# The first stage of a four-layer graph network in written order: gathers in slots, 32-pair one-hots, convolution with count blocks as weights

## The chip, the cores and the metric

One core of a Trainium2 chip runs the whole program in one launch. The metric is the device time in microseconds; three runs of the kernel before gave 3601.79, 3602.45 and 3603.7, median 3602.45.

## The reference

The graph has 6250 nodes with 64 features and 206250 edges (100000 random ones in both directions and a loop at each node), sorted by destination. Four layers follow each other, each as `x = x + layer(relu(layernorm(x)), edges)`:

```python
h = jnp.maximum(_layernorm(x, axis=-1), 0.0)
x = x + _L0_gnn_ref(h, edge_index, W3, b3, W4, b4)   # two normalised convolutions, ReLU between
h = jnp.maximum(_layernorm(x, axis=-1), 0.0)
x = x + _L1_gnn_ref(h, edge_index)                   # one convolution
h = jnp.maximum(_layernorm(x, axis=-1), 0.0)
x = x + _L2_gnn_ref(h, edge_attr_64, src, dst, ...)  # gated messages over the edges
h = jnp.maximum(_layernorm(x, axis=-1), 0.0)
x = x + _L3_gnn_ref(edge_index, h)                   # three propagations, averaged

def _sgconv(x, W, b, src, dst, n):                   # the convolution of layer 0, loops added
    norm = dinv[s] * dinv[d]                         # dinv = 1/sqrt(degree)
    agg = jax.ops.segment_sum(norm[:, None] * x[s], d, num_segments=n)
    return agg @ W.T + b
```

The last line of each layer 0 convolution shows what the stage at issue has to do: multiply features by a matrix that counts edges, scale, and apply a weight matrix.

## The kernel before

**The matrix of counts.** Nodes are padded to 6272, in 49 blocks of 128 (`NB`), seven blocks to a chunk (`CB`, `W` = 896 nodes, `NC` = 7 chunks). The first stage turns the edge list into a dense matrix of how many edges go from each source to each destination, one byte (fp8) a count, and writes it to DRAM as `A[0]` to `A[6]`. All later convolutions multiply by `A`. The features are held as three bf16 parts whose sum is the fp32 value (`split`, `U3`, `V3`), so that a matmul with counts loses nothing.

**Its steps.** `fast` computes a key for every edge, `pair` (destination times 49 plus source block; source within its block), and stores it in DRAM as `pairs`. The destinations are taken two at a time: 3136 pairs of nodes in 25 groups (`GC`) of 128. For each group, a scan over a coarse list (`near`, L804) finds roughly where each pair's edges begin (`begin`); an indirect gather on POOL brings 101 edges from there (`near2`, L872); a second scan (L876, L878) gives the exact place (`exact_i`); a second gather brings the next 128 edges (`run`, L881); they become small bf16 `digits` (L885 on DVE, L887 on ACT), which TensorE transposes (`p_dig`, L890) and DVE copies to `key` (L891). Every nine groups, comparisons (`less`, L900) and matmuls give the degrees; these make a round trip through DRAM (`degs`, `by_block`) to become `deg_dst` and `norm0`.

**Builds and strips.** `build` takes 16 pairs (`GB`): DVE writes two one-hot tiles, `hd` (block of the source, 1568 elements) and `lo` (source in its block, 2048 elements), both at L852; 16 matmuls of `lo` as weights with `hd` moving (98 columns, L861) give counts in `p_a`, two groups of eight (`SG`); ACT writes each group to a strip as fp8 (L865). A strip is 448 destinations wide (`CW`) for all 49 source blocks, 14 builds (`NQ`) fill it, and there are 14 strips (`CS`). A full strip goes to `A`.

**The first convolution.** While strip s+1 is built, `convolve(s)` multiplies strip s: the weights are the feature parts (128 sources by 64 features), the strip is the moving operand of 448 columns, and the three parts go alternately to the two halves of the result's partitions (`spread`, L748), so that the array is used as two tiles of 128*64. A matmul with the identity adds the loop edges (L949). ACT takes the result out as `y` (L957). `hidden`, in steps spread between builds, turns a finished chunk back to nodes (`twice`, L964), scales it, applies W3, ReLU and W4, and writes `V3`, the input of the second convolution.

**What sets the order.** In this stage a scheduler places the instructions of every engine by its own estimates; the text of the program is only a starting point. The second and third convolutions (`gather`, L1042) and the edge stage run with a written order on some engines (`tc.manual_schedule`). `gather` loads `piece`s of `A` (seven blocks by 896) and uses its 128x128 blocks as weights, with the 192 feature columns of a block moving. Pools of tiles have a fixed number of buffers: `rpool` 3, `opool` (one-hots) 2, `spool` (strips) 3, `p_a` 2.

Of the kernel before, what the change touches and what calls it, by code (L numbers as in the profile page):

```python
# [8 lines left out]
F32 = mybir.dt.float32  # L9
# [7 lines left out]
P = 128  # L17
N = 6250
# [572 lines left out]
GB = 16  # L591
GQ = 2
CW = 448
CS = NP // CW
SG = 8
# [21 lines left out]
def fast(ctx, tc, bad, x, src, dst, edge_attr, W3, b3, W4, b4, w1, b1, w2, b2, Bw, Bb, Cw, Cb,  # L617
# [10 lines left out]
    def strip_of(s, bs):  # L628

        return A[s // 2][:, bs, s % 2 * CW:(s % 2 + 1) * CW]  # L630
# [121 lines left out]
    nc.scalar.dma_start(X, x.rearrange("(b p) f -> p b f", p=P))  # L752
# [3 lines left out]
    with ExitStack() as ph:  # L756

        ipool = ph.enter_context(tc.tile_pool(name="ipool", bufs=1, reuse_waits="tile"))
        with ExitStack() as first:
            dpool = first.enter_context(tc.tile_pool(name="dpool", bufs=1, reuse_waits="tile"))  # L760
# [3 lines left out]
            nc.scalar.dma_start(src_i, src.rearrange("(p k) -> p k", p=P))  # L764
# [5 lines left out]
            nc.sync.dma_start(looks.rearrange("(p i) -> p i", p=P), look)  # L770
            hi = dpool.tile([P, K1], I32, name="hi")
# [7 lines left out]
            none = dpool.tile([1, 2 * (EP + 512 - E)], F32, name="none")  # L779
            nc.vector.memset(none, float(2 ** 22))  # L780
            nc.sync.dma_start(pairs[E:, :].rearrange("(o e) t -> o (e t)", o=1), none)
# [15 lines left out]
        looked = ExitStack()  # L797
        npool = looked.enter_context(tc.tile_pool(name="npool", bufs=1, reuse_waits="tile"))
        near = npool.tile([P, NS], F32, name="near")
        nc.sync.dma_start(near, looks.partition_broadcast(P))  # L800
        for c0, c1 in ((0, 3), (3, 10), (10, GC)):
            for c in range(c0, c1):
                w = min(max(int(c * 2 * P * E / N / LOOK) - 22, 0), NS - SW)
                nc.vector.tensor_scalar(junk, near[:, w:w + SW], start_of[:, c:c + 1],  # L804
                                        float(w - 1), op0=OP.is_lt, op1=OP.add,
                                        accum_out=begin[:, c:c + 1])
            nc.vector.tensor_scalar(begin[:, c0:c1], begin[:, c0:c1], float(LOOK), 0.0,
                                    op0=OP.mult, op1=OP.max)
            nc.vector.tensor_copy(begin_i[:, c0:c1], begin[:, c0:c1])
        looked.close()  # L810


        rpool = ph.enter_context(tc.tile_pool(name="rpool", bufs=3, reuse_waits="tile"))
        opool = ph.enter_context(tc.tile_pool(name="opool", bufs=2, reuse_waits="tile"))
        spool = ph.enter_context(tc.tile_pool(name="spool", bufs=3, side="right", reuse_waits="tile"))
        wpool = ph.enter_context(tc.tile_pool(name="wpool", bufs=1, reuse_waits="tile"))

        key = ipool.tile([P, 2, GC * P], BF16, name="key")
        below = ipool.tile([P, 3, GC], F32, name="below")

        W3_sb = wpool.tile([P, D], F32, name="W3_sb")
        nc.scalar.dma_start(W3_sb, W3)
        W4_sb = wpool.tile([D, P], F32, name="W4_sb")
        nc.scalar.dma_start(W4_sb, W4)
        b3_c = column(b3, 1, "b3_c")
        b4_r = rows(b4, "b4_r")
        W3T = const.tile([D, P], F32, name="W3T")
        W4T = const.tile([P, D], F32, name="W4T")

        with ExitStack() as ps:  # L830
            psum = ps.enter_context(tc.tile_pool(name="ps0", bufs=1, space=PSUM, reuse_waits="tile"))
            p = psum.tile([P, SG, P], F32, name="p_a", bufs=2)
            nc.tensor.transpose(p[:D, 0, :], W3_sb, ident)
            nc.vector.tensor_copy(W3T, p[:D, 0, :])
            p = psum.tile([P, SG, P], F32, name="p_a", bufs=2)
            nc.tensor.transpose(p[:, 0, :D], W4_sb, ident[:D, :D])
            nc.vector.tensor_copy(W4T, p[:, 0, :D])

            H0 = ipool.tile([P, NB, D], F32, name="H0")
            for c in range(NC):  # L840
                normed(H0[:, blocks(c), :], X[:, blocks(c), :])

            NQ = CW // 2 // GB
            strips = {0: spool.tile([P, NB, CW], COUNT, name="strip")}

            def build(s, q):

                at = (s * CW // 2) + q * GB
                lo = opool.tile([P, GB // GQ, 128, GQ], BF16, name="lo")
                hd = opool.tile([P, GB // GQ, 2 * NB, GQ], BF16, name="hd")  # L850
                for t, of, k in ((hd, turns, 0), (lo, count, 1)):
                    nc.vector.tensor_tensor(  # L852
                        t, of.unsqueeze(1).to_broadcast(t.shape),
                        key[:, k, at:at + GB].rearrange("p (h j) -> p h j", j=GQ)
                        .unsqueeze(2).to_broadcast(t.shape),
                        op=OP.is_equal)
                for r in range(GB // SG):
                    p = psum.tile([P, SG, P], F32, name="p_a", bufs=2)
                    for j in range(SG):
                        g = r * SG + j  # L860
                        nc.tensor.matmul(p[:, j, :2 * NB], lo[:, g // GQ, :, g % GQ],  # L861
                                         hd[:, g // GQ, :, g % GQ], start=True, stop=True)
                    col = 2 * (q * GB + r * SG)

                    nc.scalar.activation(  # L865
                        strips[s][:, :, col:col + 2 * SG].rearrange("p b (j l) -> p b j l", l=2),
                        p[:, :, :2 * NB].rearrange("p j (b l) -> p b j l", l=2), AF.Copy,
                        saturate=False)

            for c in range(GC):  # L870
                near2 = rpool.tile([P, LOOK, 2], F32, name="near2")
                nc.gpsimd.indirect_dma_start(  # L872
                    out=near2.rearrange("p e t -> p (e t)"), out_offset=None, in_=pairs[:, :],
                    in_offset=bass.IndirectOffsetOnAxis(ap=begin_i[:, c:c + 1], axis=0))
                n = rpool.tile([P, 1], F32, name="n")
                nc.vector.tensor_scalar(junk[:, :LOOK], near2[:, :, 0], start_of[:, c:c + 1], 0.0,  # L876
                                        op0=OP.is_lt, op1=OP.add, accum_out=n)
                nc.vector.tensor_add(exact_i[:, c:c + 1], begin[:, c:c + 1], n)  # L878
            for c in range(GC):
                run = rpool.tile([P, P, 2], F32, name="run")  # L880
                nc.gpsimd.indirect_dma_start(  # L881
                    out=run.rearrange("p e t -> p (e t)"), out_offset=None, in_=pairs[:, :],
                    in_offset=bass.IndirectOffsetOnAxis(ap=exact_i[:, c:c + 1], axis=0))
                digits = rpool.tile([P, 2, P], BF16, name="digits")
# [8 lines left out]
                if 0 <= c - 3 < NQ:  # L893
                    build(0, c - 3)
# [705 lines left out]
```

## Time and profile before

| | |
|---|---|
| median of the runs | 3602.45 us |
| profiled execution | 4099.17 us, its span 4097.5 us |
| granted TensorE clock, mean | 0.849 |
| busy over the span | PE 77%, PEld 53%, DVE 48%, ACT 31%, POOL 41% |
| first stage (until the first matmul of the first `gather`) | 0 to 578.4 us |
| two gathers (layer 0's second half, layer 1) | 578.4 to 1020.7 us |
| edge stage with layer 3's first sums | from about 1044 us to about 3615 us |

The profiled execution is 14% longer than the runs without a profile, so lengths of stretches are compared with its own span. PE is TensorE's matmuls and PEld its weight loads; SPq and ACTq in the timeline are DMA issues on those engines. In the timeline each row has its start, its duration, the engine and line, the operation with output and inputs, and in brackets how long the engine had been idle and what ended that. A row with a count (x12) merges consecutive instructions.

### The profile page before, as it was taken

The page shows a single profiled execution, that of the slowest core. Times are in us where ns is not written, and L with a number is a line of the kernel's source. Part 1 is how long each engine was busy: PE and PEld are TensorE (multiplying, and loading weights), DVE is VectorE, ACT ScalarE, POOL GpSimd, SP SyncE. Part 2 cuts the span into 40 slices and gives each one's busy share as a digit, 9 for nine tenths or more (in the row PEclk, how much of TensorE's full clock was granted, in tenths as well). Part 3 has the DMA queues.
Part 4 walks back from the last instruction along what each step waited for, and adds up shares of the span by engine and source line. Part 5 has one row for each costly group of instructions (what it writes and reads, how often), then busy time and mean ns, then how long its engine had stood idle before and what let it go on. Part 6 is the DMA issues. An engine that isn't in the chain of part 4 may idle for free.

```text
span 4097.5 us, 59586 instructions
## 1 busy us (share of the span) xinstructions
PE 3166.7 (77%) x24393; PEld 2174.5 (53%) x24393; DVE 1979.9 (48%) x3899; ACT 1255.6 (31%) x2024; POOL 1667.0 (41%) x1889
## 2 busy tenths in 40 slices
PE   1799999999566657776767677766767776699999
PEld 1566679998233324433434333433334443459999
DVE  6899946322244445544445444554444454561111
ACT  1577740000233333333333333333333333320000
POOL 4100010000566656656665656666566566600000
PEclk9799999999677767788777877878777787799999
DMA  3233355653322222222222222222222222136664
GB/s 101 73 84 101 94 169 190 205 181 118 95 75 61 46 53 74 61 80 57 58 63 74 64 64 67 72 59 58 75 56 61 73 65 66 45 113 194 194 203 152
DMA packets 229312, 388.76 MB, mean 95 GB/s; under 512 B 137573, under 2 KB 139743, under 8 KB 228771
## 3 DMA queue, kind: packets, MB, share of 16 engines
q1 hardware_dynamic: 170420, 321.51, 25.1%
q0 software_dynamic: 55104, 60.65, 7.9%
q8 instruction: 193, 3.16, 0.3%
q10 hardware_dynamic: 3504, 2.70, 0.3%
q14 instruction: 91, 0.75, 0.1%
HBM read 340.47 MB, written 44.24 MB: 94 GB/s over the span
## 4 chain that ended last, share of the span: by engine, by line
PE 55%; DVE 15%; another core or an unknown queue 12%; issue 9%; ACT 7%; DMA 1%; POOL 1%; DVEq 0%; ACTq 0%; SPq 0%; POOLq 0%
PE p_acc L1042 18%; PE p_sum L748 11%; PE p_bc L1396 7%; PE p L1382 6%; PE p_a L861 4%; ACT h L1386 2%; PE p_s L1424 2%; DVE m L1405 2%; DVE m L1406 2%; DVE junk L1282 2%; PE p_bc L1392 2%; PE p_e L1378 2%; PE p_sum L1276 1%; DVE m L1407 1%
## 5 line engine op out<-in xcount | busy, mean ns | idle before, releaser
L1370 POOL DMA_INDIRECT v<-Vp_dram,src_g x1616 | 1592.5, 985 | 1307.2 <-issue 786.4
L1042 PE MATMUL p_acc<-U,piece 128*128 128x192 bf16 x9604 | 814.8, 246 | 0.0
L1042 PEld LDWEIGHTS <-piece 128*128 128x128 fp8e4 x9604 | 796.4, 98 | 11.5 <-issue 4.2
L1396 PE MATMUL p_bc<-BC,h 128*128 128x256 f32 x1616 | 575.3, 485 | 22.7 <-issue 21.3
L1282 DVE SCALAR_TENSOR_TENSOR junk<-p_sum,there 128x512 bf16<-128x512 f32 (+1 forms) x392 | 241.8, 617 | 412.4 <-remote 288.6
L1405 DVE TENSOR_TENSOR m<-gate,v 128x512 f32<-128x512 f32 x202 | 140.2, 694 | 617.8 <-ACT gate L1401 426.8
L1396 PEld LDWEIGHTS p_bc<-BC,h 128*128 128x128 f32 x1616 | 335.2, 230 | 177.7 <-issue 142.0
L1276 PE MATMUL p_sum<-ident_b,piece 128*128 128x128 bf16 x1372 | 161.1, 240 | 335.8 <-DVE junk L1282 268.6
L748 PEld LDWEIGHTS <-U 128*64 128x64 bf16 x4116 | 236.9, 113 | 320.6 <-issue 179.6
L1276 PEld LDWEIGHTS <-piece 128*128 128x128 fp8e4 x1372 | 120.3, 108 | 491.4 <-issue 475.3
L748 PE MATMUL p_sum<-piece,U 128*64 128x448 fp8e4 x2058 | 273.9, 385 | 95.0 <-issue 65.5
L865 ACT ACTIVATE strip<-p_a 128x784 fp8e4<-128x784 f32 x392 | 302.0, 820 | 126.2 <-PE p_a L861 110.0
L1382 PE MATMUL p<-h,w_d 128*128 128x512 f32 x404 | 269.1, 749 | 65.9 <-ACT h L1386 56.2
L1386 ACT ACTIVATE h<-p,b_c 128x512 f32<-128x512 f32 x404 | 262.1, 684 | 186.7 <-remote 75.5
L1052 DVE TENSOR_REDUCE zg<-p_acc 128x128 f32<-128x384 f32 x112 | 56.3, 507 | 523.4 <-PE p_acc L1042 522.9
L1469 ACT ACTIVATE m<-m 128x512 bf16<-128x512 f32 x202 | 127.3, 630 | 542.6 <-DVE m L1468 368.9
L1424 PE MATMUL p_s<-m,to 128*128 128x192 bf16 x1616 | 207.4, 279 | 99.6 <-DVE r_s L1432 56.2
L1392 PE MATMUL p_bc<-BC_b,ones 3*128 3x512 bf16 x404 | 182.2, 451 | 114.7 <-DVE m L1406 97.0
L1412 ACT ACTIVATE m<-m 128x512 bf16<-128x512 f32 x202 | 127.2, 630 | 433.9 <-DVE m L1407 319.3
L1382 PE MATMUL p<-eT,w_d 128*128 128x512 f32 x404 | 246.3, 694 | 13.0 <-ACT h L1386 8.0
L1392 PEld LDWEIGHTS <-ones 3*128 3x128 bf16 x404 | 37.5, 93 | 398.7 <-issue 223.3
L748 PE MATMUL p_sum<-strip,U 128*64 128x448 fp8e4 x2058 | 244.6, 360 | 2.5 <-ACT U L711 1.4
(198 smaller groups left out, 3441.3 us busy)
## 6 DMA issues: line engine op xcount, KB each, us to landing
piece<-A SPq DMA_DIRECT2D x249, 784.0 KB
e<-in_edge_attr SPq DMA_DIRECT2D x202, 256.0 KB
A<-strip SPq DMA_DIRECT2D x14, 2744.0 KB
v<-Vp_dram,src_g POOLq DMA_INDIRECT x1616
there<-A SPq DMA_DIRECT2D x28, 784.0 KB
pairs<-pair SPq DMA_DIRECT2D x1, 1616.0 KB
Vp_dram<-v SPq DMA_DIRECT2D x7, 224.0 KB
out<-X SPq DMA_DIRECT2D x6, 224.0 KB
```

Of the source, the lines that this page charges most:

```text
L748: nc.tensor.matmul(p[half * D:(half + 1) * D, :w], U3[:, b, k, :], at_block, start=(i < 2), stop=(i >= 3 * n - 2))
L865: nc.scalar.activation(strips[s][:, :, col:col + 2 * SG].rearrange("p b (j l) -> p b j l", l=2), p[:, :, :2 * NB].rearrange("p j (b l) -> ...
L1042: nc.tensor.matmul(p[d // 2][:, d % 2 * 3 * D:(d % 2 + 1) * 3 * D], t[:, b, d * P:(d + 1) * P], U3[:, k * CB + b, :, :].rearrange("p t f - ...
L1276: nc.tensor.matmul(p[:, a - a0, :], held["here", i, k][:, a, b * P:(b + 1) * P], ident_b, start=True, stop=True)
L1282: nc.vector.scalar_tensor_tensor(junk[:, :(a1 - a0) * P], p[:, :a1 - a0, :].rearrange("p a q -> p (a q)"), 15.5, of_there, op0=OP.min, op1 ...
L1370: nc.gpsimd.indirect_dma_start(out=v[:, j, :], out_offset=None, in_=Vp_dram[:, :], in_offset=bass.IndirectOffsetOnAxis(ap=src_g[:, g, j:j ...
L1382: nc.tensor.matmul(of[g][p], w, of[g].pop(x), start=True, stop=True)
L1386: nc.scalar.activation(of[g][t], of[g].pop(p), **how)
L1392: nc.tensor.matmul(p_bc[:, 4 * b:4 * b + 4].rearrange("p j o f -> p (j o f)"), ones, BC_b, start=True, stop=False)
L1396: nc.tensor.matmul(p_bc[:, 2 * q:2 * q + 2].rearrange("p j o f -> p (j o f)"), h2[:, q * P:(q + 1) * P], BC, start=False, stop=(k == 1))
L1405: nc.vector.tensor_mul(m, of[g].pop("gate"), of[g].pop("v"))
L1424: nc.tensor.matmul(p, to[:, :, j], m3[:, j].rearrange("p t f -> p (t f)"), start=(j == 0), stop=(j == J - 1))
```

## The change

The whole first stage becomes a function, `first_stage`, run with a written order on PE, DVE, ACT and POOL (SP stays with the scheduler).

- **Loads and start.** `src` is loaded on SP's queue, behind `dst`; X alone stays on ACT's. `near` is put into the buffer of a strip and is loaded right after `looks`. Edges beyond the end get a key out of range by arithmetic (`beyond`, `pads`), so that the store of `none` no longer overlaps `pairs`.
- **Slots.** One loop of 32 slots interleaves both gathers: slot i issues the first gather of group i, scans group i-2, issues the second gather of group i-3, makes the digits of i-5 and the key of i-6. Each slot then takes 1.4 units of `fill`: the remaining scans, the layer norms in three steps (the square on ACT), then single builds (`whole`).
- **One-hots for 32 pairs.** `one_hots(s, q, 2)` writes 3136 and 4096 elements in one instruction each (`GB` = 32); `placed` does its matmuls and evictions, in two portions of 16 pairs. The one-hots of the next job are written ahead of the placing of this one.
- **Strips.** A strip is now four or three blocks of a chunk (`OF_CHUNK`), 16 or 12 portions.
- **Convolution.** `convolve` works in units of two destination blocks (or one): the strip's 128x128 block is the weight, 192 feature columns move, as in `gather`; the identity adds the loops; DVE sums the three parts out of PSUM (`tensor_reduce`). `sums(n, built)` issues n such matmuls when the strip has been built that far. `hidden` takes nodes directly: four transposes of two blocks each, and W3T in both halves of the partitions.
- `H0` lies in the buffer that `V3` takes later; `norm3` is computed after the split of U3.

```diff
-GB = 16
+GB = 32
+OF_CHUNK = ((0, 4), (4, CB))
...
+        near = new_strip().rearrange("p b w -> p (b w)")[:, :4 * NS].bitcast(F32)
...
-            nc.scalar.dma_start(src_i, src.rearrange("(p k) -> p k", p=P))
+            nc.sync.dma_start(src_i, src.rearrange("(p k) -> p k", p=P))
+            nc.scalar.dma_start(X, x.rearrange("(b p) f -> p b f", p=P))
...
+            nc.sync.dma_start(near, looks.partition_broadcast(P))
...
+        def centred(c):
...
+            nc.scalar.activation(parts["q", c], h, AF.Square)
...
+        fill = [(0.4, scanned, c) for c in range(3, 10)] + [(0.3, begun_at, 3, 10)]
+        fill += [(0.4, scanned, c) for c in range(10, GC)] + [(0.3, begun_at, 10, GC)]
+        norms = []
+        for c in range(NC + 2):
+            norms += [(1.4, centred, c)] * (c < NC)
+            norms += [(0.6, deviation, c - 1)] * (0 <= c - 1 < NC)
+            norms += [(0.8, scaled, c - 2)] * (c >= 2)
+        for _, f, *args in norms[:3]:
+            f(*args)
+        fill += norms[3:]
+        for c in range(3):
+            scanned(c)
+        begun_at(0, 3)
+
+        near_of, run_of, digits_of, credit, singles = {}, {}, {}, 0.0, 0
+        for i in range(GC + 7):
+            if i < GC:
+                near_of[i] = rpool.tile([P, LOOK, 2], F32, name="near2")
                 nc.gpsimd.indirect_dma_start(
...
+            credit += 1.4
+            while credit > 0:
+                cost, f, *args = fill.pop(0) if fill else (2.0, whole, 0, singles)
+                singles += f is whole
+                f(*args)
+                credit -= cost
...
+                p = psum.tile([P, 512], F32, name="p_sum", bufs=2)
+                nc.tensor.matmul(p[:, :m * 3 * D], ident_b,
+                                 U3[:, at:at + m, :, :].rearrange("p b t f -> p (b t f)"),
+                                 start=True, stop=False)
+                for b in range(NB):
+                    for d in range(m):
+                        nc.tensor.matmul(
+                            p[:, d * 3 * D:(d + 1) * 3 * D],
+                            strips[s][:, b, (d0 - lo + d) * P:(d0 - lo + d + 1) * P],
+                            U3[:, b, :, :].rearrange("p t f -> p (t f)"),
+                            start=False, stop=(b == NB - 1 and d == m - 1))
...
+                nc.vector.tensor_reduce(
+                    zs[c][:, d0:d0 + m, :],
+                    p[:, :m * 3 * D].rearrange("p (d t f) -> p d f t", t=3, f=D),
+                    axis=AX.X, op=OP.add)
...
+        ready = one_hots(*jobs[0], 2)
+        for c in range(NC):
+            u = wpool.tile([P, CB, D], F32, name="z", bufs=2)
+            nc.vector.tensor_mul(u, H0[:, blocks(c), :], over_features(norm0[:, blocks(c)]))
+            split(u, U3, c)
+            sums(2 * CB, built)
...
+        for k in range(0, len(jobs), 2):
+            coming = one_hots(*jobs[k + 2], 2) if k + 2 < len(jobs) else None
+            for _ in placed(*ready):
+                built += 1
+                at += 1
+                left = max(len(jobs) + 5 - at, 1)
+                sums(-(-(total - state["done"]) // left), built)
...
+                if at % 3 == 0 and layers and next(layers[0], "end") == "end":
+                    layers.pop(0)
+            ready = coming
...
+    with ExitStack() as ph, tc.manual_schedule(
+            engines={ET.PE, ET.DVE, ET.Activation, ET.Pool}):
+        norm0, norm3, V3, b4_r, hidden = first_stage(ph)
```

The later stages keep their program text.

## The prediction

> **What bounds the kernel now.** I read the page's slices first, then the first 600 us in stretches, then the order of time inside one build, then who waited. The change touches only the first stage, which ends where the gather's first matmul (L1042) starts, at 578.4 us. Stretches of that stage (columns: stretch, its length, then PE, PEld, DVE, ACT, POOL busy with instruction counts, granted clock, DMA share, GB/s):
> ```profile
> 0.00:50.00 50.00, 0.76 (x2) 0.31 (x2) 36.74 (x116) 3.41 (x9) 5.48 (x11) 1.00 0.41 123
> 50.00:100.00 50.00, 12.89 (x132) 9.78 (x132) 25.71 (x101) 12.48 (x24) 37.59 (x36) 1.00 0.29 81
> 100.00:150.00 50.00, 26.57 (x309) 21.64 (x310) 40.54 (x80) 23.04 (x40) 13.26 (x14) 0.67 0.35 95
> ...
> 200.00:250.00 50.00, 50.00 (x647) 33.08 (x648) 46.81 (x46) 36.76 (x51) 0.00 (x0) 1.00 0.31 84
> ...
> 550.00:600.00 50.00, 48.54 (x517) 35.16 (x514) 8.81 (x14) 12.84 (x20) 13.49 (x205) 1.00 0.70 236
> ```
> Three regimes show: 150 us in which no engine is full, 400 us with PE full and DVE at 94%, and a tail after 556 us in which DVE has nothing. Why it starts late stands in the timeline of POOL and DVE:
> ```profile
> 2.92 1.67 POOL L791 IOTA turns<- 128x196 bf16 x1
> 48.16 1.13 POOL L872 DMA_INDIRECT near<-pairs,begin_i  x1 [43.57 <-DVE begin L807]
> 49.59 0.96 POOL L872 DMA_INDIRECT near<-pairs,begin_i  x1 [0.31 <-issue]
> ...
> 132.90 0.95 POOL L881 DMA_INDIRECT run<-pairs,exact_i  x1 [3.92 <-ACT digits L887]
> ```
> The first gather waits 43.57 us for `begin`, which DVE computes behind all seven norms and all 25 scans, though `pairs` had landed by 26.0 (its successor on SP issues then). One gather takes 0.95 + 0.30 = 1.25 us. One build in the full regime:
> ```profile
> 549.21 1.33 PE L748 MATMUL p_sum<-strip,U 128*64 128x448 fp8e4 x12
> 549.41 0.97 DVE L852 TENSOR_TENSOR hd<-turns,key 128x1568 bf16<-128x1568 bf16 x1
> 550.30 1.22 DVE L852 TENSOR_TENSOR lo<-count,key 128x2048 bf16<-128x2048 bf16 x1
> 550.47 0.92 PE L861 MATMUL p_a<-hd,lo 128*128 128x98 bf16 x16
> 551.05 1.54 ACT L865 ACTIVATE strip<-p_a 128x784 fp8e4<-128x784 f32 x2 [0.58 <-PE p_a L861]
> 551.32 1.13 PE L748 MATMUL p_sum<-strip,U 128*64 128x448 fp8e4 x9
> ```
> From start to start, hd takes 0.89 and lo 1.13, so DVE needs 2.02 us a build. PE needs 0.85 for 16 `p_a` (550.47 to 551.32) and 1.26 or 1.07 for 12 or 9 convolution matmuls. 200 to 500 us holds 135 hd: 2.22 us a build. The waits from 180 to 560 us say who leads:
> ```profile
> DVE hd L852 <- PE p_a L861: 18.4, 33, 1.4
> ```
> DVE waits for PE, so PE leads by a little; both matter.
>
> **What the Trainium skill says.** "TensorEngine Tiling (Array Packing)", Key Properties: changing the tiling mode drains TensorE. The convolution is 128*64 here and `p_a` 128*128, so each build changes mode twice. The trace agrees: inside the bare tail, matmuls of 448 columns start every 0.093 us (114 in 10.6), so 12 make 1.12, yet `p_a` starts after 1.26: 0.14 lost, and 9, an odd count of pairs, lose 0.22. "VectorE: DVE Perf Modes", the tier table: bf16 tensor_tensor runs at 2x; the trace agrees: (1.13 - 0.89)/480 elements = 0.51 ns each, which leaves 0.07 us fixed per instruction. "TensorE: Matmul & The Clock Gate", Part 1: an idle TensorE falls to half clock. Agreed: the clock column falls to 0.5 at 120 to 160 us, and 16 `p_a` then take 1.29 from start to start.
>
> **Start.** `src` moves from ACT's queue behind X to SP behind dst (808 KB each). dst lands at 5.4 now. I estimate src at 9, and hi, src, pair, copy (0.95 + 0.95 + 1.75 + 1.0 from their rows) end at 13.6; `pairs` lands 5.3 later (20.7 to 26.0 now), at 19. SP takes looks, none, near, pairs in turn; near waits for looks and pairs for near, near 12: covered by that DVE work. DVE then has two `centred`, one `deviation`, three scans: the deviation waits for ACT's Square, which is queued behind nine loads on ACT, some of which wait for X (12.7), and a table load of 1.28: about 19.7. The first gather goes out at 22, 26 us before now.
>
> **Slots.** 32 slots interleave the 50 gathers. POOL asks 2.5 us a slot; in slots 2 to 17 DVE has near, exact, digits, key (about 0.9) and 1.3 of fill, so POOL sets 2.55: 41, plus 2 for the `less` stop. From slot 18 nine `whole` portions come in: 0.75 of near, exact and digits, then key waits for transposes behind `p_a` on PE (0.6 at full clock, 1.05 at half), 0.2, then 2.02: 3.6 to 4.0. With three lighter slots, 44. The data of gather 0 is used at 25, so the slots' last key comes at 112. Then `less`, one `whole`, deg and by_col: 7.5; the degree round trip 8.4 (146.8 to 155.2 now) covers two wholes of 4; then 2 for the root and 3.9 for the first 32-pair one-hots: 134. The split of U3 is now in strict order z, r, U. That was seen once alone (566.48 to 569.64, 3.16 us a chunk), against 11.5 us of bare DVE work: 7 x 3.1 = 22, ending at **156**. Unlike now, no builds fill its gaps. At this point 12 portions (16 pairs each) of 196 are built and 98 of 2401 sums are done.
>
> Today the split ends at 174.6 with 26 builds done (hd starts up to 171.4). So this point comes 18.6 us earlier with 14 builds less, which at 2.2 are 31: the start alone loses 12 us. Pace and tail must earn it back.
>
> **Costed at nothing.** The squares of the norms go from DVE to ACT, which idles in the slots; `beyond` and the pads lie in DVE's wait for src (5.7 to 9); the second load of W3 on ACT is in the nine loads above. W3T, W4T copies lie in the degree round trip. The 14 `y` evictions (0.54, L957) leave ACT, which is at 74%. Strips of 4 and 3 blocks are stored with a third of the DMA share taken (0.32); the next user of a buffer comes 28 portions later. If these covers failed, each is under 3 us.
>
> **Full regime.** 184 portions remain. PE: 16 `p_a` 0.86; 2303/189 = 12.2 sums at 0.083 (L1042's 255 matmuls in 21.2 us, same shape) 1.02; 28 identity sums and hidden layers 0.13: **2.01**. It loses the mode change, because both are 128*128, but also the odd pairs; against now's 2.20. A remaining switch loss is unseen: 0 to 0.14; I take 0.03. DVE: 4096 and 3136 elements at 0.51 + 2 x 0.07 = 3.87 to 3.90 for two portions, 1.95 each; the sizes are unseen, bounds 1.88 (no fixed cost left) and 2.02 (none saved). New: 28 reductions of `p_sum`, which L1052 shows as 0.56 long (0.46 to the next start): 0.07. Hidden's four 0.55 us operations for six chunks: 0.07. Sum **2.09**. ACT needs 1.54 + 0.11, below both. So DVE leads and PE is 2 to 4% behind. In written order every reduction, hidden product and split step holds the next one-hots until PE (or ACT) has come there; PE is at the end of the job whose successor is already made, so a wait is a few tenths: 28 + 6 x 3 of them, 0.2 us each, some 9 us in all, 0.05 a portion. 2.14 x 184 = 394. The norm3 root and the first job add 2. End of builds: 552.
>
> **Tail.** Now 147 convolution matmuls and three hidden steps follow the last build (556.7 to 578.4). Then: some 63 sums (5.3 us; only the last unit needs the last portion), and the first piece, queued behind the last strip's write, lands about 8 us after. SP queue order is as now. So the gather starts at 560: **18 us** before 578.4 (start -12, pace 184 x 0.08 = +15, tail +14).
>
> **Later stages.** They keep their instructions. The seventh chunk's hidden steps run inside the gather as before. I take 0 for them; cover is the gather's own 4.1 us a piece.
>
> **The base.** The profiled execution took 4099.17 us (span 4097.5, 1.7 around it), the median is 3602.45, 497 less. No view says where; 1616 gathers of the edge stage with 0.30 idle behind each would be 485. If POOL's gap is the profile's own, slots 2 to 17 shrink to DVE's 2.2, up to 6 us, but today's start, too, is partly POOL's. I carry 18 us over: 4099.2 - 18 = 4081 profiled, 3602.5 - 18 = **3584**.
>
> **Rivals.**
> A (forecast, 0.46): as above, 8 to 32 us gained.
> B (0.20): the order couples nothing: 2.09 or less a portion and slots at POOL's pace. 184 x 0.05 = 9 more, 8 from the slots, up to 8 from a shorter split: 3552 to 3570. For: ACT at 74% and PE with the drain gone leave room. Against: DVE would have to run 97% full.
> C (0.18), slower: DVE in written order waits for PE at each reduction and buffer turn, and PE then for DVE. Break-even is (578.4 - 8 - 158)/184 = 2.24 a portion, 0.10 above A. With 2.30: 11 us slower, 3613. For: two engines within 4% of each other, two buffers, strictly alternating; the switch loss of 0.14 kept would alone give PE 2.15. Against: today's loosely equal pair loses only 0.12.
> D (0.16), no change: the convolution's new shape keeps 2.21 to 2.27; pace earns only what the start loses: within 7 us of 3602.
>
> About 0.2% (7 us) is what a measurement of this kernel can tell from no change. Faster 0.66 (A and B), same 0.16, slower 0.18. The range takes A with slots at 10 us either way, B's upper half, D, and C up to a period of 2.28: 3556 to 3612.
>
> **What would show it.** Right: first gather at 20 to 25 us, first full sums at 135 to 156 with half-idle PE, 85 to 86 one-hot pairs of 3136 elements per 366 us (two portions in 4.25 to 4.35), DVE 95% and PE below 98%, gather from 550 to 570. Wrong: a first gather after 35; keys in the slots waiting over 2 us each; a period of 4.5 or more with `hd` waiting for `p_a` (C); L1042 waiting for pieces at the start; or the edge stage moving by over 10 us.

## The result: slower by 0.3%, and the profile after

The kernel after takes 3613.9 us (median of seven runs, 3608.74 to 3616.42), the kernel before beside it 3602.45 (seven, 3595.7 to 3607.07): ratio 1.0031, 95% interval 1.002 to 1.0043. The forecast was 3584. The profiles below come from one later pair of executions on one chip: before 3602.64 us (span 3601.0), after 3618.27 (span 3616.5). On some chips the edge stage of every version takes about 500 us longer, and the last key comes later (9.4 us in versions of the kernel after, 3 to 5 in before); the profile that the prediction read was of that sort, and such times (4080 to 4180 us below) are compared only with before's on the same chip.

The stretches of the first stage after (columns as in the prediction):
```profile
0.00:50.00 50.00, 2.63 (x14) 1.22 (x14) 33.97 (x136) 8.37 (x19) 23.52 (x29) 1.00 0.55 165
50.00:100.00 50.00, 15.95 (x185) 12.21 (x186) 38.79 (x115) 14.72 (x33) 33.78 (x31) 1.00 0.25 73
100.00:150.00 50.00, 23.71 (x210) 19.50 (x208) 31.07 (x52) 17.57 (x30) 0.27 (x1) 0.95 0.02 4
200.00:250.00 50.00, 45.01 (x642) 40.97 (x642) 45.88 (x30) 36.13 (x49) 0.00 (x0) 1.00 0.25 69
550.00:600.00 50.00, 37.39 (x433) 33.78 (x431) 14.55 (x17) 14.98 (x21) 9.56 (x197) 0.90 0.66 207
```
PE is no longer full from 200 to 250 us (45.0 of 50; before 50.0), but DVE, forecast at 95%, is busy only 45.9 (92%). From 100 to 150 it is busy 31.1 us. No engine is full. The early start is there, in the timeline of POOL:
```profile
2.92 1.66 POOL L819 IOTA turns<- 128x196 bf16 x1
24.47 1.12 POOL L931 DMA_INDIRECT near<-pairs,begin_i  x1 [19.89 <-DVE junk L856]
...
98.29 1.98 POOL L944 DMA_INDIRECT run<-pairs,exact_i  x1 [2.12 <-ACT digits L953]
```
The first gather goes out at 24.5 in place of 48.1 us, the last at 98.3 in place of 130.1. Where DVE loses its time later stands in the timeline round the split of one hidden chunk (L713 to L717):
```profile
304.63 1.23 PE L1035 MATMUL p_sum<-U,strip 128*128 128x192 bf16 x13
305.70 0.90 PE L894 MATMUL p_a<-hd,lo 128*128 128x98 bf16 x16
305.88 0.58 ACT L713 ACTIVATE U<-z 128x448 bf16<-128x448 f32 x1
305.90 2.28 DVE L879 TENSOR_TENSOR lo<-count,key 128x4096 bf16<-128x4096 bf16 x1
306.44 1.23 PE L1035 MATMUL p_sum<-U,strip 128*128 128x192 bf16 x13
308.10 0.61 DVE L715 TENSOR_TENSOR r<-z,U 128x448 f32<-128x448 f32 x1
308.75 0.58 ACT L716 ACTIVATE U<-r 128x448 bf16<-128x448 f32 x1 [2.29 <-DVE r L715]
309.23 2.97 ACT L898 ACTIVATE strip<-p_a 128x784 fp8e4<-128x784 f32 x4
309.36 0.62 DVE L717 TENSOR_TENSOR U<-r,U 128x448 bf16<-128x448 f32 x1 [0.64 <-ACT U L716]
309.90 1.78 DVE L879 TENSOR_TENSOR hd<-turns,key 128x3136 bf16<-128x3136 bf16 x1
310.09 0.53 PE L894 MATMUL p_a<-hd,lo 128*128 128x98 bf16 x8 [2.41 <-ACT strip L898]
```
`r` stands behind a long `lo` on DVE; ACT waits 2.29 us for it, with evictions (L898) queued behind its copy; PE waits 2.41 for these, and DVE 0.64 in the next step. PE alone would be quick: 13 sums take 1.07 from start to start, 16 `p_a` 0.74. What DVE waits for between 155 and 560 us (total, times, longest):
```profile
DVE hd L879 <- PE p_a L894: 11.5, 14, 1.7
DVE z L1086 <- PE p_node L1082: 4.6, 3, 1.9
DVE U L717 <- ACT U L716: 3.9, 6, 0.6
DVE z L1042 <- PE p_sum L1035: 3.4, 3, 1.7
DVE r L715 <- ACT U L713: 3.1, 2, 1.5
```
These are 26.5 us; all of DVE's waits in before, in the same window, are 19.6, of which 18.4 are `hd` waiting for `p_a`. The tail, in the timelines of SP and PE:
```profile
568.04 0.51 SPq L905 DMA_DIRECT2D A<-strip  x1
568.66 14.20 SPq L1142 DMA_DIRECT2D piece<-A  x7
...
573.34 0.33 PE L1145 MATMUL p_acc<-zeros,ident_b 128*128 128x384 bf16 x1
583.30 2.42 PE L1148 MATMUL p_acc<-U,piece 128*128 128x192 bf16 x14 [9.63 <-DMA piece<-A]
```
PE is ready at 573.3 and waits 9.63 us for the first piece, queued on SP behind the last strip's store; then 14 matmuls take 2.42 us in place of 1.32. In before, on the same chip, the pieces stand behind the store as well, but PE is at work on the convolution until the first is there:
```profile
556.57 0.51 SPq L1010 DMA_DIRECT2D A<-strip  x1
557.18 29.21 SPq L1036 DMA_DIRECT2D piece<-A  x9
...
575.13 0.54 PE L748 MATMUL p_sum<-strip,U 128*64 128x448 fp8e4 x2
...
575.77 1.32 PE L1042 MATMUL p_acc<-U,piece 128*128 128x192 bf16 x14
```

**Where the 11 us are.** On this chip:

| | before | after | difference |
|---|---|---|---|
| U3 split ends | 172.2 | 151.2 | -21.0 |
| one-hots made by then, in portions of 16 pairs | 26 | 14 | 12 fewer, at 2.26 us: +27.1 |
| from there to the last eviction, per remaining portion | 384.3/170 = 2.26 | 416.8/182 = 2.29 | 182 x 0.03 = +5.4 |
| last eviction's end to the gather | 19.2 | 15.3 | -3.9 |
| gather starts | 575.8 | 583.3 | +7.5 |
| its two passes | 442.6 | 444.8 | +2.2 |

Together +9.7; the medians differ by 11.5, the two executions of the table by 15.6. From the gathers' end to the end of the span before took 2582.6 us, after 2588.4 here and 2579.0 in its first profile: this scatters by more than what is missing.

The third row is not a slower pace. From one `hd` to the next, over all but the last job, both kernels take the same, 2.245 and 2.247 us a portion. The 5 us are at the two ends: 4.1 us in place of 1.9 from the split's end to the next `hd`, and a last job of two portions, which takes 8.2 us from its `hd` to its last eviction where before's last one, a single portion, takes 5.3.

### The profile page after: what moved, and what is told of

It is laid out like the page before. It is cut to its first block, busy times and chain, and to the rows that moved or that the text cites. A ratio compares the mean times of both kernels' runs of the same rounds, so it can differ in the third digit from the quotient of the medians.

```text
span 3609.4 us, 59472 instructions
## 1 busy us (share of the span) xinstructions
PE 3009.5 (83%) x24477; PEld 2211.7 (61%) x24477; DVE 1957.3 (54%) x3738; ACT 1237.2 (34%) x2011; POOL 1662.2 (46%) x1889
## 4 chain that ended last, share of the span: by engine, by line
POOL 33%; PE 28%; issue 13%; DMA 7%; DVE 6%; ACT 2%; DVEq 0%; POOLq 0%; SPq 0%; ACTq 0%
POOL v L1476 33%; PE p_acc L1148 21%; DMA v<-Vp_dram,src_g 7%; PE p_sum L1035 2%; PE p_sum L750 1%; PE p_a L894 1%; PE p_bc L1502 1%; DVE lo L879 1%; DVE hd L879 1%; ACT strip L898 1%; DVE m L1511 0%; DVE m L1512 0%; DMA piece<-A 0%; PE p_acc L1145 0%; PE p_node L741 0%
## 5 line engine op out<-in xcount | busy, mean ns | idle before, releaser
L1502 PE MATMUL p_bc<-BC,h 128*128 128x256 f32 x1616 | 589.4, 499 | 0.0
L1502 PEld LDWEIGHTS p_bc<-BC,h 128*128 128x128 f32 x1616 | 344.1, 236 | 158.3 <-issue 118.9
L1518 ACT ACTIVATE m<-m 128x512 bf16<-128x512 f32 x202 | 127.2, 630 | 801.7 <-DVE m L1513 801.7
L898 ACT ACTIVATE strip<-p_a 128x784 fp8e4<-128x784 f32 x392 | 299.8, 821 | 130.0 <-PE p_a L894 122.2
L1488 PE MATMUL p<-h,w_d 128*128 128x512 f32 x404 | 258.0, 725 | 36.5 <-ACT h L1492 36.5
L750 PE MATMUL p_sum<-piece,U 128*64 128x448 fp8e4 x2058 | 239.7, 375 | 26.2 <-DVE junk L1388 17.9
L1035 PE MATMUL p_sum<-U,strip 128*128 128x192 bf16 x2401 | 241.3, 252 | 21.3 <-ACT strip L898 14.8
L894 PE MATMUL p_a<-hd,lo 128*128 128x98 bf16 x3136 | 193.8, 215 | 56.1 <-DVE lo L879 40.6
L1035 PEld LDWEIGHTS <-strip 128*128 128x128 fp8e4 x2401 | 201.4, 100 | 38.5 <-ACT strip L898 21.1
L879 DVE TENSOR_TENSOR lo<-count,key 128x4096 bf16<-128x4096 bf16 (+1 forms) x104 | 224.9, 2163 | 0.0
L894 PEld LDWEIGHTS <-lo 128*128 128x128 bf16 x3136 | 171.3, 101 | 80.2 <-DVE lo L879 51.6
```

The lines of the kernel that those rows point to most:

```text
L750: nc.tensor.matmul(p[half * D:(half + 1) * D, :w], U3[:, b, k, :], at_block, start=(i < 2), stop=(i >= 3 * n - 2))
L879: nc.vector.tensor_tensor(t, of.unsqueeze(1).to_broadcast(t.shape), key[:, k, at:at + n * 2 * SG].rearrange("p (h j) -> p h j", j=GQ) .uns ...
L898: nc.scalar.activation(strips[s][:, :, col:col + 2 * SG].rearrange("p b (j l) -> p b j l", l=2), p[:, :, :2 * NB].rearrange("p j (b l) -> ...
L1035: nc.tensor.matmul(p[:, d * 3 * D:(d + 1) * 3 * D], strips[s][:, b, (d0 - lo + d) * P:(d0 - lo + d + 1) * P], U3[:, b, :, :].rearrange("p ...
L1488: nc.tensor.matmul(of[g][p], w, of[g].pop(x), start=True, stop=True)
L1502: nc.tensor.matmul(p_bc[:, 2 * q:2 * q + 2].rearrange("p j o f -> p (j o f)"), h2[:, q * P:(q + 1) * P], BC, start=False, stop=(k == 1))
```

## The experiments

Lengths are of the first stage. "Intervals" means the sum of the 90 intervals from one 32-pair `hd` to the next: 407.0, 403.8 and 404.4 us in three profiles of after, of which 90 x 3.90 = 351 are the one-hots themselves.

**Before, unchanged (two runs).** Both met the long edge stage.

> The kernel before, unchanged, for a second trace. Theory 'the edge stage has two paces': in the trace shown ahead of the prediction the edge stage took 2570 us, in the trace of the changed kernel 2068; if that is a state of the edge stage and not of the kernel, this trace has the edge stage near 2070 and a span near 3600, and the first gather again begins at 578 to 580 us. Rival 'the change made the edge stage faster and something else slower': the edge stage is again 2500 us or more here.

> The kernel before, unchanged, for a profile in the same state as the one of the kernel after (an edge stage of about 2070 us). The two kernels differ by 11 to 12 us in their times; the gather of sums starts 582.2 to 585.6 us in the kernel after, and 578.4 in the earlier profile of before, taken where the edge stage was 500 us longer. Theory (the whole difference is made ahead of the end of the gathers): here the gather starts at 571 to 576 us, its two passes last 442 us against 444.5, and from their end to the end of the span both kernels take the same to within 4 us. Rival (the stages that the change does not touch give part of it, since they start at another time against the clock or the transfers): the gather starts at 578 to 581 as in the earlier profile, and the later stages are 4 to 8 us shorter in before.

4170.22 and 4102.68 us; the gather starts at 581.0 and 580.85. Both kernels have the short edge stage in the pair of the table and versions of both have the long one elsewhere, so it does not come from the change; for a comparison on one chip there is that pair.

**Hidden's steps set apart.** Each operation of `hidden` on ACT or DVE that reads another engine's output comes one or two portions later, and a step is taken at every portion in place of every third. One of the gaps:
```diff
-                if at % 3 == 0 and layers and next(layers[0], "end") == "end":
+                if layers and next(layers[0], "end") == "end":
...
             r = stat.tile([P, CB, D], F32, name="r")
             nc.vector.tensor_sub(r, z, u3[:, :, 0, :])
+            for _ in gap(2):
+                yield
             nc.scalar.activation(u3[:, :, 1, :], r, AF.Copy)
```


> The changed kernel, with the hidden layer's work cut finer: each ACT or DVE operation that reads what another engine makes is written one or two portions after it, one step at every portion. Theory 'order': ACT stands at the split's copy behind DVE's 4 us of one-hots, and the strip evictions stand behind ACT; of the 31 us that DVE idles among 90 jobs about 18 go, and the time falls from 3614 to about 3596, with the six intervals that hold the split at 4.97 instead of 5.7 to 7.35. Rival 'the engines are simply full': the idle moves to other jobs, less than 5 us gained.

Intervals 388.5 us, against 404.5 in the trace with the moved store (below), which is from the same chip and leaves this order as it is: 16.0 less. The six with a split take 4.90 in the mean in place of 6.25, which is half of the gain. DVE's waits from 165 to 552 us:
```profile
DVE hd L879 <- PE p_a L894: 8.6, 12, 0.9
DVE z L1042 <- PE p_sum L1035: 2.3, 2, 2.1
```
The waits at the splits and at L1086 have vanished; those for `p_a` are shorter too. The stall is real, and about 16 us of it come from where the steps stood. The times (4144.38 us, ratio to before 0.9992, 0.9957 to 1.0026) are with the long edge stage and can't be set against after's.

**Sums only on portions placed two or more ago.**
```diff
-                sums(-(-(total - state["done"]) // left), built)
+                sums(-(-(total - state["done"]) // left), built - 2)
```


> The changed kernel, with sums allowed only on portions that were placed at least two portions ago. Theory 'order': TensorE's 36 us of waits for ACT's evictions at the sums vanish from the waits, but most lie beside DVE's work; 4 to 10 us gained, 3604 to 3610. Rival: the waits only cover for a late DVE; within 3 us of 3614, and TensorE waits for the one-hots instead.

Intervals 395.4 us, 9.0 less than the same 404.5. PE's waits for a strip at the sums (14.9 us at L1035 in after) left the list; it waited longer for `lo` instead (28.6 and 17.4 us on weight loads and matmuls, against 19.7 and 11.4 in the trace with the moved store). So the theory's 4 to 10 us are there, and what the rival said of PE is true as well. Time 4157.74, ratio 1.0032 (1.0004 to 1.006), again with the long edge stage: no gain over before shows in it.

**The last strip stored from ACT's queue.**
```diff
-                        nc.sync.dma_start(strip_of(s, slice(0, NB)), ...)
+                        if s < CS - 1:
+                            nc.sync.dma_start(to, frm)
+                        else:
+                            nc.scalar.dma_start(to.bitcast(F32), frm.bitcast(F32))
```


> The changed kernel, with the last strip stored from ACT's queue instead of SP's. Theory 'tail': the first pieces wait behind that store on one queue (first gather matmul at 585.6 us, 9.7 us after TensorE was free); from another queue they share the DMA engines with it and the gather begins at about 579: 5 to 8 us gained, 3606 to 3609. Rival 'bytes': store and pieces together keep the DMA engines full whichever queue they come from, so the gather begins no earlier than 583 and 0 to 2 us are gained.

Its timelines of SP, ACT and PE:
```profile
569.52 10.16 SPq L1145 DMA_DIRECT2D piece<-A  x4
...
576.08 0.76 ACTq L909 DMA_DIRECT2D A<-strip  x1
...
581.53 1.32 PE L1151 MATMUL p_acc<-U,piece 128*128 128x192 bf16 x14
```
The pieces are asked for before the store; the gather starts 5.5 us after the last eviction (15.3 in after), without a wait and with 14 matmuls in 1.32 us: 9.8 us, more than the 5 to 8 expected. Intervals 404.5. Time 4139.05 (long edge stage), ratio 0.9968 (0.9936 to 1.0001).

**After, unchanged**, as the base of the next three on the same chip.

> The kernel after, unchanged, run beside the others: the first stage of each of them is read against this one. In the earlier profile of it the gather of sums starts at 585.6 us, the 90 intervals from one 32-pair hd to the next sum to 407 us, and the last eviction of a strip is 15.3 us ahead of the gather. If those three belong to the kernel's order and not to the chip, they are the same here to within 2 us, whatever the edge stage's pace is; if they follow the clock[...], the stage is longer by some per cent.

3611.15 us; gather at 582.2, last eviction 566.1, intervals 403.8. The three lengths repeat within 3.4 us, not within 2.

**ACT alone left to the scheduler.**
```diff
-            engines={ET.PE, ET.DVE, ET.Activation, ET.Pool}):
+            engines={ET.PE, ET.DVE, ET.Pool}):
```


> ACT's order alone is left to the scheduler, in the whole stage; PE, DVE and POOL keep the order that is written. Theory that ACT's written order carries the stalls (the second copy of a split stands behind the first eviction of the round while its r is still waiting for DVE): the scheduler puts the copies where their inputs are there, and the six intervals with L715 and L717 (6.26 us in the mean) fall towards 5, the sum of the 90 by some 8 to 15 us. Rival (a chain of data in a written order of DVE and PE is what takes the time, whatever ACT's order is): the sum stays at 407 within 4 us. A third case, that the scheduler's order puts copies ahead of evictions whose portions are done, makes it longer.

3605.52 us (one execution), intervals 402.3, the six split intervals 5.96 in place of 6.25, gather at 581.6 against 582.2. The rival holds: ACT's order alone is not what loses the time. `r` still stands behind `lo` in DVE's written order. DVE's or PE's order alone left to the scheduler was not tried.

**The split of U3 pipelined.** The next chunk's product is placed ahead of this chunk's second step.
```diff
-            split(u, U3, c)
-            sums(2 * CB, built)
+            # z and first copy of chunk i; r and second copy of i-1; last part and sums of i-2
```


> Only the loop that splits U3 is changed: the first product of a chunk is placed ahead of the second of the chunk before it, so that DVE does not wait for ACT's copy inside a chunk. In the kernel after a chunk takes 3.07 us, of which DVE waits 2 x 0.64 for ACT. Theory (the loop is on the path from the node degrees to the last strip, since DVE is at the bound from there on): the loop from the first z to the last U falls from 21.6 us to 13 or 14, and the gather of sums starts 8 us earlier than in the kernel after. Rival (PE has portions and sums to catch up at this point, so that DVE's gain is waited away in the next intervals): the loop is shorter by 8 but the gather starts less than 3 us earlier, and the intervals after the loop are longer by the difference.

3606.8 us (one execution); the loop takes 12.0 in place of 21.6 us, the intervals stay (404.6), and the gather starts at 574.3, 7.9 earlier. The theory holds: DVE is on the path there.

**All four mends, written order kept.**

> All the mends of the theory in one kernel: the hidden layer's steps set apart by a portion each, the sums taken only over portions placed two rounds ago, the last strip's store issued from ACT's queue, and the split of U3 pipelined over its seven chunks (z of the next chunk ahead of the r of this one). Theory (the time is lost in waits between DVE, ACT and PE inside the written order, and in the queue of the last store): intervals 407 down by 18.5 for the steps and by up to 11.6 for the lag, so 377 to 389; after the last eviction 15.3 down to 5.5; split of U3 shorter by 8. Sum: the gather of sums starts 36 to 48 us earlier than in the kernel after, so the time is 25 to 36 us below before on a chip where before and after differ by 11.5. Rival (the waits of the order replace each other, the pace is held by DVE and by the evictions anyway): intervals no shorter than 388, the gather only 20 to 30 us earlier.

3576.44 us (3568.8 to 3582.14) against before's 3598.66: ratio 0.9933 (0.9915 to 0.995). Intervals 385.1 (-18.7), last eviction to gather 7.6 (-8.6), split as above; gather at 546.4, 35.8 earlier, at the lower edge of the theory. The time is 22 us below before, less than the 25 to 36 expected. The store, the split and the pace add up almost as they stand alone; the steps and the lag do not (18.7 together, not 16 + 9): there the rival is half right.

**The same with four more portions ahead of the split.**
```diff
-            credit += 1.4
+            credit += 1.4 if i < GC - 3 else 2.0
...
-        for _ in range(2 + len(jobs) % 2):
+        for _ in range(3 + (len(jobs) + 1) % 2):
```


> All the mends of e5_all, and four more portions built ahead of the split of U3: three in the last slots of the gathers (100 to 125 us, where DVE is busy 14.8 of 25 us in e5_all and POOL is done), one more while the degrees go to memory and back. Theory (before had 26 portions built when its split ended, after 12, and each portion missing costs DVE 1.95 us later): each of the four is saved at the end, less what it delays the last key by, so the gather starts 4 to 8 us earlier than the 546.4 of e5_all, and the time is 3569 to 3573, 0.8% below before. Rival (the slots' short steps are delayed as much as the builds save): the last key is 4 to 8 us later, and the time stays at 3576.

Met the long edge stage: 4092.63 us, ratio 0.9927 (0.9902 to 0.9952), no different from the 0.9933 of the kernel without them. The last key came at 125.1 us, against 119.8 in after's variants there, and the first 32-pair `hd` 9.4 later: what four portions save (two jobs, 7.8 us of one-hots) the time up to that `hd` loses. The rival holds: in written order a build in a slot delays the next key.

**16 pairs at a time again.**
```diff
-GB = 32
+GB = 16
-        ready = one_hots(*jobs[0], 2)
+        ready = one_hots(*jobs[0], 1)
```


> The one-hots are made for 16 pairs at a time again, with a look-ahead of one portion, all else as in the kernel after. Two 16-pair jobs cost DVE about 0.15 to 0.2 us more than one of 32 pairs (2.0 against 1.95 us a portion), so 184 portions cost it some 12 us more. Theory A (long instructions on DVE are what its short ones, the splits and reductions, queue behind, and so what ACT and PE wait for): the plain waits and the split intervals halve, so the sum over 180 portions is 395 to 409, not above the 404 to 407 of after. Theory B (the waits come from the order of PE and ACT, not from the length of DVE's block): waits as before and 12 us more, 415 to 422.

4180.36 us (one execution, long edge stage). From 200 to 500 us a portion takes 2.328 us, against 2.255 in after: 13 us over 180 portions. Over the whole stretch it is more, 2.372 against 2.247 with the moved store on a chip of the same sort, some 22 us, and the gather starts at 611.2. DVE's idle time between 180 and 560 us is 30 us, against 26 in after. Theory B holds in kind, and theory A fails: the waits do not shrink, so long instructions alone are not their cause, and the 32-pair one-hots, with the longer look-ahead that comes with them, are a gain.

**The written order taken off the whole stage.**
```diff
-    with ExitStack() as ph, tc.manual_schedule(
-            engines={ET.PE, ET.DVE, ET.Activation, ET.Pool}):
+    with ExitStack() as ph:
```


> The first stage's written order is taken off as a whole: the same instructions, put in order by the scheduler on PE, DVE, ACT and POOL. It puts builds of strips far earlier, among the gathers of the degrees. Theory (what the written order couples is what ate the gain): the gather of sums starts 5 to 20 us earlier than the 582 to 586 of the kernel after. Rival (the written order is needed: left alone, builds of strips delay the short steps between the gathers of pairs on POOL, so that the last key and the degrees come later): the last key comes after 120 us instead of 110, the split of U3 after 160, and the gather starts later than in after.

Gather at 543.9 with the long edge stage (4083.05 us, one execution), last key at 109.4, where after's versions had it at 119.8. With the moved store, on a chip of the same sort, the last eviction was at 576.1; here it is at 528.6, 47 us earlier. That is more than any single mend; the rival (keys delayed by builds) fails.

**Pair on one chip, and the order taken off with the store moved.** The last two kernels differ in six more portions called for among the gathers (`credit += 1.4 if i < 18 else 2.1`).

> The kernel before, beside the kernel after on the same chip. Theory (the whole difference is made ahead of the gather of sums): the gather starts 9 to 15 us earlier than in after, and from there to the end of the span the two kernels differ by less than 4 us on a chip with the short edge stage. Rival: the gather starts within 8 us of after's, and the rest of the difference lies in stages that the change does not touch. On a chip with the long edge stage the gather starts at 578 to 581 as in the earlier profiles.

> The kernel after on the same chip. If the chip has the short edge stage, the last key comes at 110.4 and the gather starts at 582 to 586, as in the earlier profiles. If it has the long one, the variants run there so far had their last key 9.4 us later: then 120, and the gather at 592 to 595.

> The written order taken off as in e7_sched, and the last strip stored from ACT's queue as in e3_store, all else as in the kernel after. Theory (the written order is the part of the change that loses the time, the other parts gain): e7_sched's gather starts 40 us or more ahead of after's, and the store takes 9 to 10 us off the 16 us between the last eviction and the gather, so the gather starts at 532 to 537 and the time is 1.0 to 1.4% below before. Rival (e7_sched's early start was of that one execution or is given back later): within 0.5% of before.

> As e11_schedstore, with 18 in place of 12 portions of 16 pairs called for among the gathers of the degrees; in e7_sched DVE is busy 25 of 50 us from 50 to 100 us. Theory (a portion built where DVE is idle saves its 1.95 us later): the gather starts 8 to 12 us earlier than in e11_schedstore, 0.2 to 0.3% of the time. Rival (the builds push the keys and the degrees back, or DVE's idle time there is used already): within 3 us of e11_schedstore, or later.

Before 3602.64 and after 3618.27 us are the pair of the table: the gather starts 7.5 apart, on the rival's side of its bound. The part after the gathers differs by 5.8, within its own scatter, so whether it adds to the loss stays open.

Without written order and with the store moved: **3555.9 us** (3551.14 to 3556.97) against 3605.03 for before, ratio 0.9866 (0.985 to 0.9883). This beats both kernels. Its stretches, and its tail on PE:
```profile
50.00:100.00 50.00, 19.03 (x210) 14.68 (x209) 33.49 (x111) 15.95 (x33) 35.84 (x34) 1.00 0.28 82
100.00:150.00 50.00, 38.95 (x497) 35.25 (x495) 49.25 (x62) 32.57 (x49) 0.00 (x0) 0.76 0.24 67
200.00:250.00 50.00, 46.56 (x689) 43.27 (x687) 49.91 (x32) 38.51 (x52) 0.00 (x0) 1.00 0.36 89
```
```profile
517.46 6.76 PE L1038 MATMUL p_sum<-U,strip 128*128 128x192 bf16 x80
524.06 0.33 PE L1147 MATMUL p_acc<-zeros,ident_b 128*128 128x384 bf16 x1
524.22 1.32 PE L1150 MATMUL p_acc<-U,piece 128*128 128x192 bf16 x14
```
DVE is busy 49.25 of the 50 us in which it had 31.07, and 49.91 from 200 to 250. All of its waits from 115 to 510 us:
```profile
DVE hd L879 <- PE p_a L894: 5.2, 11, 1.0
```
The gather starts 59.1 us ahead of after's on the same chip: at 151 us 26 portions are made in place of 14 (12 x 1.95 = 23), two portions take 4.255 in place of 4.510 us between 200 and 500 us (85 times: 22), and the tail is 5.4 in place of 15.3 us (10). That makes 55 of the 59. The 12 portions have two sources: the last key comes at 102.0 in place of 110.7 and the split ends at 137.0 in place of 151.2, and the scheduler builds while the split runs, with `z`, `r` and `U` of other chunks between the long one-hots. The gather is 8 us ahead of the 532 expected from the run on the slower sort of chip, where the last key came 7.4 later.

Six more early portions: 3565.56 us, ratio 0.9891 (0.9874 to 0.9907), gather at 526.2. The rival holds here as well: the last key is 2.5 us later, the split ends 13.7 later (150.7), and two portions take 4.49 in place of 4.39 us over the whole of the 32-pair jobs. The medians are 9.7 us apart, the starts of the gather only 2.0; the rest lies behind it, and its cause is open, like that of the later split.

## Why the prediction was wrong, step by step

- **Start: nearly right.** First gather 24.5 (forecast 22), last key 110.7 (112), end of U3's split 151.2 (156), the split itself 21.6 (22), 12 portions placed as counted. The balance "18.6 us earlier with 14 builds less" is the right form, but it sets portions placed against one-hots made; like with like, on one chip, it is 21.0 earlier with 12 fewer, a loss of 6, not 12.
- **Full regime: the work was priced well.** PE's 2.01 a portion was rather too high: 16 `p_a` take 0.74 in place of 0.86, and 13 sums take 1.07, which is 13 x 0.083, so nothing is lost between the two any more. (Whether the mode change had been the reason is not tested apart: the shape of the matmuls changed with it.) DVE's 1.95 is exact, 3.90 for two, though the sum as printed, with 0.51 ns, makes 3.83; with 0.52, which fits the medians of before (0.886 and 1.135 us), it makes 3.90. The reductions, 0.46 each, were right too.
- **Full regime: the waits, the step that failed, with the tail.** The mis-sized term is the stall: "0.2 us each, some 9 us in all", 0.05 a portion. It is 26.5 us between 155 and 560, 0.15 a portion. Of these, 15.0 are at the points that were priced, the reductions, hidden products and splits; 11.5 are `hd` waiting for `p_a`, which the forecast put at nothing because PE was to be 2 to 4% behind. The priced points came out too cheap because every wait was sized from PE at the end of a job. ACT is named there ("or ACT") and then set aside as "below both" by load, yet it stands in the same chain: `lo` holds `r`, `r` holds ACT's copy, the copy holds the evictions, these hold PE, and PE holds `hd`. Setting the steps apart took 16 us back.
- **So the gain of pace is missing.** From `hd` to `hd` it is 2.247 a portion where before has 2.245, in place of 2.14. Forecast +15 us; measured none, and 5 lost at the two ends of the stretch.
- **Tail: right about the sums, wrong about the transfer.** "The first piece lands about 8 us after": it was 15.3. In before the same queue order was hidden by PE's convolution behind the last build; that cover is what the change removed. Forecast +14, measured +4.
- **The sum.** Against the forecast's own times the split ends 5 us early, the stretch to the last eviction takes 416.8 in place of 396 (21 late), and the tail 15.3 in place of 8 (7 late): the gather starts at 583.3 in place of 560.
- **Costed at nothing.** The wait lists show no stall of its own at the loads, the squares on ACT or the strips' stores in mid-stage. The later stages were not quite free: the first matmuls of the gather ran slow after PE's idle time, 2 us in all.
- **The base.** "No view says where" the 497 us are: POOL's wait list does. Before with the long edge stage, then with the short one, from 1030 to 3620 us:
```profile
POOL v L1370 <- DVE m L1405: 492.4, 101, 14.3
POOL v L1370 <- DVE m L1405: 0.3, 1, 0.3
```
POOL's 0.30 between two gathers is in both, so the guess that it makes the difference is wrong. It did not move the forecast's difference, but the start of before's gather was taken 2.6 us late.
- **The rivals.** C is what happened: slower by 11 us, at a pace just above its break-even of 2.24, with its own sign ("a period of 4.5 or more with `hd` waiting for `p_a`": 4.51) and that of L1042 waiting for pieces. It was given 0.18. Its mechanism is right in part: the buffer turn is the largest wait, 11.5 us, but the reductions are only 3.4; 11.6 went through the hidden products and the splits, with ACT in the chain, and the tail adds its share. D's pace (2.21 to 2.27) came true as well, but not its "within 7 us". That the strict order could be worth less than the scheduler's, about 49 us (59.1 less the store's 9.8), was nowhere in the range of cases. What the slots or the convolution's new shape are worth alone was not tried.

## What to carry to other kernels

When a written order replaces a scheduler's, cost the idle time that the scheduler was filling, stretch by stretch: here DVE was busy 31 of 50 us in a stretch where 49 were possible. In a strict order follow each short step through every queue it stands in, also on an engine that is lightly loaded; here `r`, behind a `lo` of 2.28 us on DVE, was waited for on ACT and on PE, and then on DVE again. And when work is moved out of a tail, ask what transfer it was covering.

## What the hardware showed unasked

After 9.63 us of waiting PE took 2.42 and 2.45 us for its next two groups of 14 matmuls, then 1.32. From the issue of a strip's store of 2352 KB, with a piece of 784 KB behind it on the same queue, to the use of the piece it took 15.3 us; with the store on another engine's queue, the piece asked for first was in time. One kernel, one core: its edge stage differs by 500 us between chips, nearly all of it POOL waiting for buffers that DVE frees late (492.4 us against 0.3), and the last key by 9 us in versions of the kernel after, by 3 to 5 in before. The version left to the scheduler had its last key 10 us earlier than the written order on the slower sort of chip, and 8.7 earlier, with the store moved, on the faster. Why DVE is late on the slower sort stays open.
